# A fifth block of quantized rows, and a piece of that work in every unit of the second attention

## Chip, cores and metric

The kernel is written in Tile, a layer that derives the semaphores from the data flow and plans the order of each engine's instructions itself. It runs on one core of one Trainium2 chip. The metric is the time of one execution on the device, in microseconds (us); a kernel is stated by the median of its runs.

## What is computed

The reference is a two-layer gated Flamingo stack on x of shape (2, 2048, 512), which the kernel sees as 8 blocks of 512 tokens (4 per sequence), each block four tiles of 128 tokens.

```python
x = x + tanh(g_xattn[0]) * L0_xattn(layernorm(x), ctx)   # 16 heads of 32
x = x + tanh(g_ffn[0])   * L0_ffn(layernorm(x))          # 256 routed tokens of a sequence
x = x + tanh(g_xattn[1]) * L1_xattn(layernorm(x), ctx)   # 16 heads of 64: the "second attention"
x = x + tanh(g_ffn[1])   * L1_ffn(layernorm(x))          # the BitNet feed-forward
...
def L1_ffn(x):
    h = bit_linear(x, w1)            # 512 -> 2048: rows to 8-bit integers, weights ternary
    h = silu(depthwise_conv1d(h))    # over neighbouring tokens, kernel of 3
    return bit_linear(h, w2)         # 2048 -> 512: the rows of h to 8-bit integers again
```

What the change touches is the quantization in the last line, that of the "inner rows" h: each token's row of 2048 values is scaled by 127 over its largest absolute value and rounded to integers.

## The kernel before, in words

**The stages in time.** First attention with the router beside it (to about 520 us), the rest of the routed attention and feed-forward (to about 760 us), the second attention (760 to 1560 us), and the second half of the BitNet feed-forward (to the end).

**The second attention** (`cross_attention`, line 218, called on line 1397) is a loop over units (line 353): 16 units u per block n, one unit per head, 128 units and 12 more that empty the pipeline. A unit makes scores (L279), a softmax (maximum on VectorE L119, exponentials on ScalarE L122, reciprocal L130 on VectorE, product L131 on GpSimd), the transposes of the probabilities of two units earlier (L297, copied by VectorE L298), every fourth unit the values (L305) and, in units with u % 4 = 1, the queries of the next group of heads (L256, 16 matmul records, in two chunks that ScalarE moves out, L268). The output projection of a block (L328, moved out by VectorE L339) is spread over eight units of the next block. Each unit ends with a call `beside(u)`, here `beside4` (line 1295).

**What runs beside it.** When a block's attention is done, `stage3_done` (line 1304) queues two generators on the list `stream`: `quantize_rows` and `first_half` (line 1200; the up projection L1179 and the convolution L1189 to L1196, four channel groups k, each ending in a store of the 1 MB tile h to `h_d[g]`, L1227). `first_half` queues `scales_of` (line 1245) on the list `ending`; that computes the rows' scales `hid_s` and, for blocks g below `EARLY`, queues `integers(g)` on the list `later` (L1257). `beside4` takes two steps of `ending` and of `stream` in a unit, and one step of `later` unless u % 4 = 1.

**`integers(g)`** (line 1267) spreads the block's scales over the partitions (four transposes L82 on TensorE, a copy to the single tile `s_b` L1264 on ScalarE) and then takes 16 pieces, one step each. A piece is a column tile of 128x512 of h: a load `hf` from `h_d` (L1272), a product with `s_b` on VectorE (L1279), the rounding, on VectorE in even pieces (L1285, one instruction) and on ScalarE in odd ones (L1282 and L1283, two passes), and a store of the bf16 result to `hq_d[g]` (L1286). The tiles `hf` and `hi` have two buffers each. All of these transfers are issued by SyncE (SP), whose queue is in order.

**The second half** begins when the last block's values are done (`second_half_starts`, line 1344). A loop over blocks g and their tiles i (line 1454) calls `down_and_out` (line 1405): 16 matmuls of `hq` with w2 into one bank of PSUM (L1409), the product with the row's factor and the addition of x on VectorE (L1412), the store. After each tile it takes three steps of `behind`, the generator `quantize_hidden(g + 1)` (line 1355), which provides the integers of the next block. For blocks below `EARLY` these are eight loads from `hq_d` (L1369), whose tiles `hq` have 24 buffers, those of three blocks. For the others `quantize_hidden` does the work of a block in place: 16 loads from `h_d` (L1376; the last block's columns were kept in SBUF), the spreading of the scales, 16 products on VectorE (L1385), 4 roundings on VectorE (L1391) and 12 times two passes on ScalarE (L1388, L1389). The up projection and convolution of the last block, g = 7, are finished in the first three blocks of this loop (`beside4(None, 1)`, line 1477). The two single tokens at the ends of the sequences (`last_tokens`) add 32 matmuls.

```python
def beside4(u, share=2):
    for _ in range(share):
        advance(ending)
        advance(stream)
    if u is None or u % 4 != 1:
        advance(later)
```

The order on each engine is Tile's: it plans with modelled durations, in the order of the program where several instructions are ready. An instruction can stand earlier on its engine than the program has it.

Of the kernel before, what the change touches and what calls it, by code (L numbers as in the profile page):

```python
# [43 lines left out]
def flamingo_kernel(ctx: ExitStack, tc: tile.TileContext, a: dict, out: bass.AP):  # L44
# [1059 lines left out]
    hid_f = const.tile([P, NT], F32, name="hid_f")  # L1104
    h_d = [dramp.tile([P, HC, BLK], F32, name=f"h_d{g}") for g in range(B * NBLK)]
    LAST = B * NBLK - 1
    EARLY = 4
    hq_d = [dramp.tile([P, HC, BLK], BF16, name=f"hq_d{g}") for g in range(EARLY)]
    x3_d = [dramp.tile([S, D], F32, name=f"x3_d{b}") for b in range(B)]

# [134 lines left out]
    def scales_of(g, amax):  # L1245
# [9 lines left out]
        nc.vector.tensor_scalar(hid_f[:, ts(g, TB)], inv, finstep, None, ALU.mult)  # L1255
        if g < EARLY:
            later.append(integers(g))  # L1257
# [9 lines left out]
    def integers(g):  # L1267


        def load(c):  # L1270
            h = act4.tile([P, BLK], F32, name="hf", tag="hf", bufs=2)
            nc.sync.dma_start(out=h, in_=h_d[g][:, c, :])  # L1272
            return h

        s_b, h = scales_spread(g), load(0)
        for c in range(HC):
            behind = load(c + 1) if c + 1 < HC else None
            yield
            nc.vector.tensor_tensor(h, h, s_b, ALU.mult)  # L1279
            q = act4.tile([P, BLK], BF16, name="hi", tag="hi", bufs=2)  # L1280
            if c % 2:
                nc.scalar.activation(h, h, AF.Copy, bias=RND)  # L1282
                nc.scalar.activation(q, h, AF.Copy, bias=-RND)  # L1283
            else:
                nc.vector.tensor_scalar(q, h, RND, RND, ALU.add, ALU.subtract)  # L1285
            nc.sync.dma_start(out=hq_d[g][:, c, :], in_=q)  # L1286
            h = behind

    stream, later = [], []

    def advance(q):
        while q and next(q[0], q) is q:
            q.pop(0)

    def beside4(u, share=2):


        for _ in range(share):
            advance(ending)
            advance(stream)  # L1300
        if u is None or u % 4 != 1:
            advance(later)

    def stage3_done(n, tiles):
        for i, t in enumerate(tiles):
# [49 lines left out]
    def quantize_hidden(g):  # L1355
# [8 lines left out]

        if g < EARLY:
            for k in range(HC // GQ):
# [30 lines left out]
    cross_attention(  # L1397
        W1, act, hold, ps_mm, psum_pool(units, "L1_sc", 3), psum_pool(units, "L1_o", 2), row,
        1, 10, stage3_rows, stage3_done, beside4, second_half_starts,
    )  # L1400
    right1.close()
# [52 lines left out]
    for g in range(LAST + 1):  # L1454
        if g == LAST - 1:
            while stream or ending:
                beside4(None)
            last = last_tokens()
        behind = quantizing[1] if g == 0 else quantize_hidden(g + 1) if g < LAST else iter(())
        for i in range(TB):  # L1460
            t, r, p = ahead.pop(0)
            down_and_out(
                lambda c: hq[g][c // GQ][:, c % GQ, ts(i, P)],
                hid_f[:, g * TB + i : g * TB + i + 1],
                P,
                t,
                out[ds(g // NBLK * S + r, P - p), :],
                p,
                nc.sync if g == LAST else nc.gpsimd,
            )  # L1470
            if g < LAST:
                ahead.append(row_tile(g + 1, i))
            if g >= LAST - 1:
                next(last, None)
            for _ in range(3):
                next(behind, None)
                beside4(None, 1)
# [65 lines left out]
```

## Time and profile before

| | |
|---|---|
| median of the runs | 1743.49 us (3 runs, 1741.15 to 1747.48) |
| the profiled execution | 1741.68 us, its span 1740.0 us |
| mean granted TensorE clock | 0.982 of full speed |
| busy: TensorE matmul, VectorE, ScalarE, GpSimd | 94%, 71%, 63%, 32% of the span |
| second attention, blocks 2 to 6 | 103.8 to 108.3 us each |
| second half, first to last matmul of L1409 | 1563 to 1736 us |

The page of a profile gives first the busy time of each engine, then the span in 40 equal slices (here of 43.5 us) with the busy tenths of each engine, then the DMA queues, the chain of work that ended last, and groups of equal instructions with their mean duration and the idle time in front of them. PE is TensorE's matmuls, PEld its weight loads, DVE VectorE, ACT ScalarE, POOL GpSimd, SP SyncE. The trace behind it answers for single lines, tiles and stretches of time.

### The profile page before, as it was taken

Reading aid. Unit: us, or ns where it says so; the run is one execution under the profiler, and the core shown is the slowest. Engines: PE = TensorE matmul, PEld = TensorE weight load, DVE = VectorE, ACT = ScalarE, POOL = GpSimd, SP = SyncE. Lnnn points to the kernel's source line nnn. Section 1 sums busy time; section 2 is a strip of 40 time slices with the busy share of each in tenths; the row PEclk is TensorE's granted clock in tenths of the full one; section 3 lists DMA queues with packets and bytes.
Section 4 is the critical chain, followed back from the end, with each engine's and each line's share of the span. In section 5 each row is a group of like instructions: output and inputs, shape, how many; then the busy total and the mean of one; then the engine's idle time right before and its main releaser. Section 6 shows DMA issues by size and latency. Waiting matters only on the chain.

```text
span 1740.0 us, 25223 instructions
## 1 busy us (share of the span) xinstructions
PE 1628.8 (94%) x8076; PEld 856.4 (49%) x8122; DVE 1240.6 (71%) x2576; ACT 1103.3 (63%) x3170; POOL 560.1 (32%) x703
## 2 busy tenths in 40 slices
PE   7999888899999989999999999999999999998988
PEld 4545444455555665755454544445444454444433
DVE  5566777865757543345368889898789889877986
ACT  2876566456553333345267878788787887855575
POOL 2534443442340021033223243343332333343221
PEclk9999999999989999999999999999999999999999
DMA  6011111121005851920011334234133233157294
GB/s 222 7 68 56 37 62 68 61 67 55 25 37 197 274 174 63 300 85 25 19 55 73 122 99 148 92 115 164 73 128 115 88 103 132 78 217 264 100 311 149
DMA packets 116973, 196.99 MB, mean 113 GB/s; under 512 B 13117, under 2 KB 51517, under 8 KB 113129
## 3 DMA queue, kind: packets, MB, share of 16 engines
q1 hardware_dynamic: 110664, 177.54, 29.5%
q0 software_dynamic: 5888, 17.83, 3.2%
q8 instruction: 64, 1.05, 0.2%
q14 instruction: 69, 0.56, 0.1%
q10 hardware_dynamic: 288, 0.00, 0.0%
HBM read 120.89 MB, written 74.45 MB: 112 GB/s over the span
## 4 chain that ended last, share of the span: by engine, by line
PE 48%; DVE 27%; ACT 9%; issue 6%; DMA 6%; POOL 3%; SPq 0%; DVEq 0%; POOLq 0%; ACTq 0%
PE pp L328 12%; PE pq L256 9%; DVE h L1196 4%; PE po L305 4%; PE tp L297 4%; PE sc L279 4%; ACT A L122 3%; PE ph L1179 3%; DVE nmx L119 2%; DVE marks L873 2%; DVE u L1190 2%; DVE AT L298 1%; DMA x<-h_d 1%; DVE L_ln_st L99 1%; DMA h_d<-h 1%
## 5 line engine op out<-in xcount | busy, mean ns | idle before, releaser
L122 ACT ACTIVATE A<-sc,nmx 128x128 f32<-128x128 f32 x1024 | 364.7, 386 | 122.6 <-DVE nmx L119 117.9
L131 POOL TENSOR_TENSOR A<-A,rden 128x512 f32<-128x512 f32 x256 | 280.5, 1098 | 493.9 <-DVE rden L130 402.4
L328 PE MATMUL pp<-L_wo,OT 128*128 128x512 f32 x768 | 360.8, 601 | 5.4 <-DVE x L339 5.4
L256 PE MATMUL pq<-xnT,L_wq 128*128 128x512 f32 x768 | 344.8, 596 | 1.3 <-DVE x L339 1.2
L122 ACT ACTIVATION_READ_ACCUMULATOR A<-sc,nmx 128x1 f32 x1024 | 229.5, 224 | 0.0
L256 PEld LDWEIGHTS pq<-xnT,L_wq 128*128 128x128 f32 x768 | 142.5, 191 | 159.7 <-issue 151.4
L119 DVE TENSOR_REDUCE nmx<-sc 128x4 f32<-128x512 f32 x256 | 168.7, 679 | 67.7 <-PE sc L279 67.6
L328 PEld LDWEIGHTS pp<-L_wo,OT 128*128 128x128 f32 x768 | 134.9, 191 | 148.9 <-issue 130.9
L1196 DVE SCALAR_TENSOR_TENSOR h<-u,cw,h 128x512 f32<-128x512 f32 x256 | 197.2, 803 | 5.8 <-ACT h L1192 5.3
L297 PE MATMUL tp<-ident,A 128*128 128x128 f32 x1024 | 164.8, 285 | 23.5 <-POOL A L131 12.4
L297 PEld LDWEIGHTS tp<-ident,A 128*128 128x128 f32 x1024 | 118.6, 143 | 93.2 <-issue 47.5
L298 DVE COPY AT<-tp 128x512 f32<-128x512 f32 x192 | 130.0, 679 | 38.7 <-PE tp L297 38.1
L279 PEld LDWEIGHTS sc<-L_kT,qT 32*128 32x128 f32 (+1 forms) x2048 | 109.7, 189 | 70.8 <-issue 58.2
L279 PE MATMUL sc<-L_kT,qT 32*128 32x128 f32 (+1 forms) x2048 | 136.2, 291 | 3.7 <-ACT A L122 3.1
L1192 ACT ACTIVATE h<-u,cb,cw 128x512 f32<-128x512 f32 x128 | 99.5, 809 | 62.1 <-DVE u L1190 57.1
L305 PE MATMUL po<-AT,L_v 128*32 128x512 f32 (+1 forms) x512 | 120.1, 655 | 11.5 <-DVE AT L298 11.1
L1409 PE MATMUL po<-w2q,hq 128*128 128x512 bf16 x501 | 117.6, 381 | 9.8 <-ACT hq L1389 6.2
L1179 PE MATMUL ph<-xiT,w1q 128*128 128x512 bf16 x477 | 122.5, 379 | 2.1 <-DVE u L1190 0.2
L1190 DVE TENSOR_TENSOR u<-ph,inv_b 128x512 f32<-128x512 f32 x128 | 85.4, 683 | 31.5 <-PE ph L1179 27.7
L130 DVE RECIPROCAL rden<-den 128x4 f32<-128x4 f32 x256 | 43.6, 170 | 80.3 <-ACT A L122 72.7
L1189 POOL COPY u<-carry 128x2 f32<-128x2 f32 x112 | 44.3, 397 | 150.3 <-DVE h L1196 127.7
L1179 PEld LDWEIGHTS <-w1q 128*128 128x128 bf16 x512 | 49.2, 98 | 79.1 <-issue 35.3
(246 smaller groups left out, 2383.1 us busy)
## 6 DMA issues: line engine op xcount, KB each, us to landing
h_d<-h SPq DMA_DIRECT2D x28, 1024.0 KB, 3.9
x_d<-x SPq DMA_DIRECT2D x64, 256.0 KB, 2.0
hf<-h_d SPq DMA_DIRECT2D x64, 256.0 KB, 3.0
x<-h_d SPq DMA_DIRECT2D x48, 256.0 KB, 5.3
x<-in_x SPq DMA_DIRECT2D x32, 256.0 KB, 3.7
x_d<-xo SPq DMA_DIRECT2D x32, 256.0 KB, 2.0
xf<-x_d SPq DMA_DIRECT2D x32, 256.0 KB, 3.5
x<-x_d SPq DMA_DIRECT2D x32, 256.0 KB, 3.4
```

Of the source, the lines that this page charges most:

```text
L119: nc.vector.tensor_reduce(nmx, sc, AX.X, ALU.max, negate=True)
L122: nc.scalar.activation(out_tile[:, h, :], sc[:, h, :], AF.Exp, bias=nmx[:, h : h + 1], accum_out=den[:, h : h + 1],)
L131: nc.gpsimd.tensor_tensor(out_tile, out_tile, rden.unsqueeze(2).to_broadcast([P, n, width]), ALU.mult,)
L256: nc.tensor.matmul(pq, W.wq[:, d, ts(e, P)], xnT[:, d, :], start=(d == 0), stop=(d == DC - 1),)
L279: nc.tensor.matmul(sc[h][:, t, :], qT[e % cpg][r, ts(t, P)], W.kT[r, b, e, :], start=True, stop=True,)
L297: nc.tensor.transpose(tp[:, t, :], A[:, t, :], ident)
L298: copy(AT, tp.rearrange("p t n -> p (t n)"))
L305: nc.tensor.matmul(po[h * dh : (h + 1) * dh, :], W.v[:, b, ts(hd, dh)], AT[c * hpc + h], start=True, stop=True,)
L328: nc.tensor.matmul(pp, OT[e][:, ts(i, P)], W.wo[:, e, :], start=(e == 0), stop=(e == nE - 1),)
L1179: nc.tensor.matmul(ph, w1q[:, d, ts(c, P)], xiT[g][:, d, :], start=(d == 0), stop=(d == DC - 1),)
L1190: nc.vector.tensor_tensor(u[:, 2:], ph, inv_b[g], ALU.mult)
L1196: nc.vector.scalar_tensor_tensor(z, u[:, ds(k, BLK)], cw[:, c, k : k + 1], z, ALU.mult, ALU.add)
```

## The change

One constant is raised and one condition is taken away.

```diff
@@ -1104,7 +1104,7 @@
     LAST = B * NBLK - 1
-    EARLY = 4
+    EARLY = 5
     hq_d = [dramp.tile([P, HC, BLK], BF16, name=f"hq_d{g}") for g in range(EARLY)]
@@ -1298,8 +1298,7 @@
         for _ in range(share):
             advance(ending)
             advance(stream)
-        if u is None or u % 4 != 1:
-            advance(later)
+        advance(later)
```

With `EARLY = 5` block 4 too is quantized by `integers(4)` beside the second attention, by way of `hq_d[4]`, a new tensor in DRAM of 2 MB, and `quantize_hidden(4)` becomes eight loads. With the condition gone, each unit takes a step of `later`, also the units in which queries are made. No tile in SBUF or PSUM changes its size or number.

## Prediction

> **What bounds the kernel now.** I read the page first (busy shares and the 40 slices), then busy time by block of the second attention, then the groups and waits of the last 83 us.
>
> ```profile
> PE 1628.8 (94%) x8076; PEld 856.4 (49%) x8122; DVE 1240.6 (71%) x2576; ACT 1103.3 (63%) x3170; POOL 560.1 (32%) x703
> ...
> PE   7999888899999989999999999999999999998988
> ...
> DVE  5566777865757543345368889898789889877986
> ACT  2876566456553333345267878788787887855575
> ```
>
> TensorE is busy nearly everywhere. VectorE is at 8 or 9 tenths in slices 22 to 35, the second attention, so what is put there must be weighed, not assumed free. The two places of the change are the attention (work added) and the end (work removed).
>
> Busy time for blocks 2 to 6 of the second attention, each window from the first exponential of a block to that of the next:
>
> ```profile
> 901.00:1008.30 107.30, 105.10 (x462) 51.75 (x465) 85.31 (x156) 81.60 (x198) 34.02 (x53) 0.98 0.26 92
> 1008.30:1114.60 106.30, 101.75 (x457) 50.94 (x461) 93.72 (x176) 85.81 (x208) 38.05 (x55) 0.98 0.32 111
> 1114.60:1218.40 103.80, 102.09 (x451) 50.17 (x455) 94.48 (x178) 87.67 (x209) 39.97 (x54) 1.00 0.39 132
> 1218.40:1326.70 108.30, 103.54 (x461) 51.27 (x464) 92.61 (x173) 86.18 (x207) 35.80 (x53) 1.00 0.33 115
> 1326.70:1430.50 103.80, 100.91 (x459) 50.77 (x463) 87.16 (x159) 83.69 (x204) 35.54 (x54) 1.00 0.26 92
> ```
>
> Columns: length, then PE, PEld, DVE, ACT, POOL busy (and count), clock, DMA share, GB/s. And the products of the pieces (L1279) in the same windows, so that one sees how many pieces each block held:
>
> ```profile
> 901.00:1008.30 107.30, 3.78 (x5) 0.98 0.26 92
> 1008.30:1114.60 106.30, 8.67 (x11) 0.98 0.32 111
> 1114.60:1218.40 103.80, 12.51 (x16) 1.00 0.39 132
> 1218.40:1326.70 108.30, 11.00 (x14) 1.00 0.33 115
> 1326.70:1430.50 103.80, 6.18 (x8) 1.00 0.26 92
> ```
>
> PE is busy 97 to 98% of these blocks and its idle time adds up to 16 us in 530. Five pieces or sixteen, the block takes the same: 107.3, 106.3, 103.8, 108.3, 103.8 us for 5, 11, 16, 14 and 8 pieces. The attention is bound by TensorE.
>
> The last 83 us (1657 us to the end) look different:
>
> ```profile
> L1385 DVE TENSOR_TENSOR x<-x,s_b 128x512 f32<-128x512 f32 x48 | 31.2, 687 | 8.2 <-DMA x<-h_d 7.0 <-ACT s_b L1264 0.9 <-ACT hq L1389 0.2
> L1409 PEld LDWEIGHTS <-hq 128*128 128x128 bf16 x268 | 24.0, 98 | 45.1 <-ACT hq L1389 19.0 <-DVE hq L1391 2.8 <-issue 0.4
> ```
>
> There TensorE waits for integers: its weight loads sat idle 19.0 us for ScalarE's rounding and 2.8 us for VectorE's. The copies of `s_b` (L1264) that open the four blocks quantized in place start at 1657.6, 1674.1, 1691.7 and 1709.4 us, so a block costs 16.5 to 17.7 us, while its 64 matmuls need 13.8 (the 32 single-token ones ran in 7.07 us, 0.216 each). Before 1657 us VectorE finishes the convolution of block 7, and TensorE runs blocks 0 to 3 from stored integers: it is at block 4's first weight load at 1660.0 us.
>
> **Part 1, the end: block 4's quantization is removed.** What goes, from the rows above and of L1388, L1389, L1391: 16 products of 0.69 and 4 roundings of 0.42 on VectorE, 24 passes of 0.62 to 0.63 on ScalarE (15 us), one copy of `s_b`, 16 loads of 256 KB in a stretch with a DMA share of 0.84 to 0.94. What comes: 8 loads of 256 KB from `hq_d` (L1369, median 7.1 us to landing). They need the buffers of block 1, free at about 1627 us when TensorE goes on to block 2; the loads of block 3 were issued the same way, over 40 us before use. From 1625 to 1650 us the DMA share is 0.20, so they have room.
>
> Then two limits. The chain of quantization has three links instead of four: block 7's last rounded column, now needed at 1725.4 us, comes 17.7 us earlier, at 1707.7, and with the 10.8 us that TensorE needed after it (1725.4 to 1736.2) that would be 1718.5. TensorE's own work from 1660.0: 256 matmuls and 32, at 0.216, are 62.2 us, and three spreads of scales at 0.49 make 63.7: 1723.7. TensorE is the later one, so **the most that can go is 1736.2 - 1723.7 = 12.5 us**. What is late next: block 6's integers. At full pace block 6 would start at 1660.0 + 27.6 = 1687.6, but its last columns are rounded at about 1692.8 (they follow the products that now end at 1690.5 and 0.69), and its first tile can't end before about 1693 instead of 1691. I take 2 us of loss; **10.5 us go**.
>
> **Part 2, the attention: sixteen pieces are added.** Following the generators, `integers(0)` now runs in units 42 to 58, 1 to 74, 2 to 90, 3 to 106 and 4 to 122, each begun in the unit in which its scales are ready; before, four blocks took units 42 to 127. All fits into the 140 units, so nothing is left for the emptying loop on line 1451. Added: VectorE 16 x 0.682 + 8 x 0.416 = 14.2 us; ScalarE 16 x 0.63 + 0.57 = 10.7 us; TensorE four transposes, 0.6 us; SP 16 x 0.425 + 16 x 0.32 = 11.9 us of issuing, for 6 MB more.
>
> Bounds: above, VectorE's whole 14.2 us, if it set the pace. Below, -3 us, since blocks differ by 4.5 us with no relation to pieces, and another order may fall out better. Between them I compare like with like, units 4 to 7 of each block (convolution, queries and output projection at once), where VectorE is 92 to 98% busy when pieces are there. Without pieces (blocks 2 and 6) 34.3 and 33.6 us; with 5 or 6 pieces (3, 4, 7) 34.4, 35.0, 35.0; block 5, with 6, 39.8. Without block 5 that is 0.85 us for 5.3 pieces, 0.16 each, 2.6 us for 16; with it 0.38 each, 6.1 us. I take **2.6 us**, as the block that held 16 pieces was among the fastest. The cover is TensorE's matmuls; if it is gone, the price is 14.2.
>
> The other edit, a piece in units with u % 4 = 1, adds a wait: an odd piece's two passes (1.26 us) or an even piece's 1.1 us on VectorE stand ahead of the maxima (L119), the exponentials (L122) and the copies of queries (L268) queued behind them, and the next scores wait for those. Such a unit has 16 query matmuls on TensorE (7.1 us in a row at 1248 us), a cover that other units lack, so I cost it at nothing beyond the 2.6; its full price is rival 3. On SP each piece's load and store stand in order with the loads and stores of the attention's rows and of h; a load (median 3.0 us to landing) was awaited 14 times for 17.3 us in all by VectorE, not by TensorE. The transposes of `s_b` now follow the scales at once in five blocks instead of one: in block 0 TensorE idled 0.66 us for it; four more are 2.6 us at most, within the 6.1 above.
>
> A rule that speaks against the change: in this trace 16 of the 78 softmax products on GpSimd (L131) between 985 and 1500 us overlap a piece's product on VectorE, and take 1198 ns instead of 1077. The Trainium skill (GPSIMD Engine Reference, section 1, Specifications) says that GpSimd shares its SBUF interfaces with VectorE and contends with instructions that have two SBUF inputs or use both ports. Row and rule agree; by the row, sixteen more products lengthen GpSimd by 16 x 0.12, some 2 us, at 32% busy; by the rule alone, were GpSimd held for each whole product, 11 us, still beside TensorE.
>
> **Sum.** -10.5 + 2.6 = -7.9 us on the profiled execution's 1741.68: 1733.8. That execution stands 1.8 us below the median of the runs, 1743.49; against the median the same step gives 1735.6, and I forecast 1735.5.
>
> **Rivals.**
> 1. *TensorE is reached in full and the attention charges nothing.* Single-token matmuls fill the wait for block 6, and another order of pieces is as good as that of block 4. For it: 16 pieces in 103.8 us. Against: no block's order repeats. -12.5, down to -15.5 with the -3: 1728 to 1731.
> 2. *The attention takes back most of it.* Stalls like that of block 5's units 4 to 7 (5 us) come once or twice more, or VectorE, at 97% there, gives way. 6.1 to 10 us: net -4.4 to -0.5, 1739 to 1743.
> 3. *Slower: the units with queries become the bound.* Pieces fall in 20 such units (45 to 121). If each holds up the softmax and queries queued behind it by its 1.1 to 1.26 us and TensorE has nothing else to run, 20 x 1.2 = 24 us come in, and 10.5 go: +13.5, 1757; half of it +1.5. It decides from about 0.8 us per unit (+5.2). Against: TensorE's long cover there, and an order planned across units.
> 4. *The change doesn't do what it says:* block 4's stored integers come no earlier than rounded ones. In the second half SP sat 53 us in one wait at L1376, for a buffer, until about 1660. If the eight loads stand behind such a wait, they land 7 us later, TensorE starts block 4 at about 1667, and 10.5 shrinks to 3.5: net -0.9, 1742.6. Against: in the program they come before the loads of block 5.
>
> **How the numbers follow.** About 0.3%, 5.2 us, is what a measurement of this kernel can tell from no change. Forecast 0.45 (its own range 1732 to 1738), rival 1 0.17, rival 2 0.18, rival 4 0.07, rival 3 0.13. Faster is the first two, 0.62; within 0.3% rivals 2 and 4, 0.25; slower rival 3, 0.13. The range leaves out rival 1's lowest end and most of rival 3: 1728 to 1750.
>
> **What would show it.** Right: blocks 3 to 7 of the attention at 104 to 108 us with 14 to 18 products of L1279 each; three `s_b` copies after 1650 us instead of four, 16 to 18 us apart; block 4's 64 matmuls in about 14 us with no wait for ScalarE; last matmul at about 1726 plus what the attention added. Wrong: blocks of the attention over 109 us with VectorE at 95% or more (rivals 2, 3); weight loads of L1409 waiting for `hq_d` loads (rival 4); a first matmul of the second half later than 1563 by more than 6 us.

## The result, and the profile after

The changed kernel takes **1746.97 us** (median of 21 runs) against 1743.49 us, with a ratio of 1.0025 [1.0013, 1.0037]. It is slower by a quarter of a per cent, less than the bound of 0.3% but with an interval that excludes a gain. The forecast was 1735.5, faster. The profiled execution takes 1743.53 us, its span 1741.8 (before: 1740.0), its mean granted clock 0.984. Lines behind L1301 stand one lower than before.

From the page of the changed kernel, busy times and VectorE's slices:

```profile
PE 1633.7 (94%) x8078; PEld 862.3 (50%) x8122; DVE 1246.0 (72%) x2580; ACT 1095.7 (63%) x3162; POOL 564.3 (32%) x703
...
DVE  5566777865667542444368898997989978878886
```

VectorE's total is only 5 us higher: work has moved, as intended. Busy time by block of the second attention, in the same columns as before, each window from the first exponential of a block to that of the next:

```profile
897.40:1003.10 105.70, 103.50 (x463) 51.65 (x465) 85.30 (x156) 81.47 (x199) 34.01 (x53) 1.00 0.26 94
1003.10:1110.80 107.70, 105.11 (x461) 52.55 (x464) 94.89 (x178) 87.44 (x212) 38.48 (x54) 1.00 0.37 126
1110.80:1221.70 110.90, 105.76 (x458) 52.82 (x460) 96.74 (x177) 87.57 (x211) 39.35 (x54) 1.00 0.36 124
1221.70:1330.50 108.80, 104.12 (x455) 51.90 (x458) 97.83 (x181) 87.88 (x212) 38.74 (x55) 1.00 0.37 128
1330.50:1437.00 106.50, 103.85 (x456) 51.41 (x460) 93.80 (x172) 87.27 (x211) 38.08 (x54) 1.00 0.35 119
```

The blocks now hold 6, 16, 16, 17 and 17 products of L1279. They last 105.7 to 110.9 us; before, 103.8 to 108.3. VectorE is at 87 to 90% in the four full ones, no more than the fullest block before (91%). The clock column reads 1.00 everywhere, where two windows of before read 0.98, so two blocks of before were slowed by the clock and none of these was.

The stretches of the two profiled executions, cut at the first query matmul of the second attention, at the first weight load of the second half, and at the last matmul:

| stretch | before | after | difference |
|---|---|---|---|
| second attention | 816.4 | 827.6 | +11.2 |
| of it lost to the halved clock | 10.2 | 5.1 | -5.1 |
| attention without that loss ("net") | 806.2 | 822.5 | +16.3 |
| second half, to its last matmul | 173.0 | 165.8 | -7.2 |

The loss is half the length of the stretches in which the granted clock was 0.5. The attention began 2.3 us earlier in the second trace, and small differences behind the last matmul make up the rest of the +1.8 in the span.

Where in a block the attention has grown is seen when blocks 3 to 6 are cut by units, as the working did it for units 4 to 7 (us net of the clock, summed over the four blocks, and pieces in them):

| units of a block | 0 to 3 | 4 to 7 | 8 to 15 |
|---|---|---|---|
| before | 108.4, 13 pieces | 142.8, 17 | 169.3, 19 |
| after | 109.2, 22 pieces | 140.7, 16 | 184.0, 26 |

So 14.7 of the 16.3 us lie in units 8 to 15 of these blocks. That is where the spread of a block's scales now stands right behind the scales, which before was so in block 2 alone. Before, block 2's units 8 to 15 took 44.9 us and those of blocks 3 to 6 took 42.0 to 43.0, the 42.0 with eight pieces; after, the latter take 44.9 to 47.1, with six or seven.

In the end, the groups of products in place and of weight loads:

```profile
L1384 DVE TENSOR_TENSOR x<-x,s_b 128x512 f32<-128x512 f32 x32 | 20.6, 685 | 4.8 <-DMA x<-h_d 2.5 <-ACT s_b L1264 1.6 <-ACT hq L1388 0.6
L1408 PEld LDWEIGHTS <-hq 128*128 128x128 bf16 x512 | 50.0, 99 | 65.3 <-ACT hq L1388 6.2 <-issue 3.2
```

Sixteen products are gone, and the wait of the weight loads for ScalarE's rounding fell from 19.0 to 6.2 us. The `s_b` copies after 1650 us are three, at 1674.0, 1691.0 and 1707.1. TensorE in the stretch ahead of the first of them:

```profile
1666.84 0.65 PE L1251 MATMUL pm<-ident,amax 128*128 128x128 f32 x4 [0.17 <-DVE amax L1234]
1667.33 6.21 PE L1408 MATMUL po<-w2q,hq 128*128 128x512 bf16 x28
1673.37 0.60 PE L81 MATMUL pb<-ident,hid_s 128*128 128x128 f32 x4
1673.81 13.50 PE L1408 MATMUL po<-w2q,hq 128*128 128x512 bf16 x59
1689.45 0.39 PE L1408 MATMUL po<-w2q,hq 128*128 128x512 bf16 x1 [2.14 <-ACT hq L1388]
```

Here block 5's scales could be spread (`pb`) as soon as block 7's are done (`pm`), but 28 matmuls stand between the two on TensorE. In those 6 us ScalarE stands before its copy of `s_b` (9.9 us in that wait), and at 1689.45 TensorE waits 2.14 us for integers that ScalarE rounds too late.

### The profile page after: what moved, and what is told of

The parts are those of the page before. It is cut to its first block, busy times and chain, and to the rows that moved or that the text cites. A ratio compares the mean times of both kernels' runs of the same rounds, so it can differ in the third digit from the quotient of the medians.

```text
span 1741.8 us, 25266 instructions
## 1 busy us (share of the span) xinstructions
PE 1633.7 (94%) x8078; PEld 862.3 (50%) x8122; DVE 1246.0 (72%) x2580; ACT 1095.7 (63%) x3162; POOL 564.3 (32%) x703
## 4 chain that ended last, share of the span: by engine, by line
PE 50%; DVE 29%; ACT 9%; DMA 5%; issue 3%; POOL 3%; SPq 0%; POOLq 0%; DVEq 0%; ACTq 0%
PE pp L328 10%; PE pq L256 9%; DVE h L1196 5%; PE po L305 4%; ACT A L122 4%; PE tp L297 4%; PE sc L279 3%; PE ph L1179 3%; DVE nmx L119 2%; PE pu L659 2%; DVE marks L873 2%; PE pw L659 2%; PE acc L644 2%; PE po L1408 2%; DVE u L1190 2%
## 5 line engine op out<-in xcount | busy, mean ns | idle before, releaser
L256 PEld LDWEIGHTS pq<-xnT,L_wq 128*128 128x128 f32 x768 | 142.2, 190 | 163.3 <-issue 151.8
L1196 DVE SCALAR_TENSOR_TENSOR h<-u,cw,h 128x512 f32<-128x512 f32 x256 | 192.6, 785 | 2.6 <-ACT h L1192 2.2
L279 PEld LDWEIGHTS sc<-L_kT,qT 32*128 32x128 f32 (+1 forms) x2048 | 114.9, 189 | 73.4 <-issue 57.3
L279 PE MATMUL sc<-L_kT,qT 32*128 32x128 f32 (+1 forms) x2048 | 143.6, 291 | 5.7 <-ACT A L122 5.4
```

The lines of the kernel that those rows point to most:

```text
L256: nc.tensor.matmul(pq, W.wq[:, d, ts(e, P)], xnT[:, d, :], start=(d == 0), stop=(d == DC - 1),)
L279: nc.tensor.matmul(sc[h][:, t, :], qT[e % cpg][r, ts(t, P)], W.kT[r, b, e, :], start=True, stop=True,)
L1196: nc.vector.scalar_tensor_tensor(z, u[:, ds(k, BLK)], cw[:, c, k : k + 1], z, ALU.mult, ALU.add)
```

## The experiments

Two traces show where the time is, not why the attention is longer. These theories are named by letters in what was expected. **N**: the number of pieces, whose work is charged wherever it stands. **P**: their place in the last units of a block (in the last pair of runs, P is the plan). **Q**: the units with queries. **S**: scales spread at once. **F**: blocks with more than 12 pieces. **L**: the late spread in the end, above. **R**: score matmuls taken apart. **W**: small waits. **V**, **A**: the pieces' work on VectorE, on ScalarE. **O**: the order and waits that come with a step, whatever its work.

All results; ratios are to the kernel before on the same chip, stretches are from one profiled execution each:

| run | median us, ratio [95%] | attention, lost, net | second half |
|---|---|---|---|
| e1_rate4 | 1749.13, 1.0042 [1.0020, 1.0064] | 822.3, 5.1, 817.2 | 178.0 |
| e2_count5 | 1747.53, 1.0045 [1.0022, 1.0068] | 814.2, 6.8, 807.4 | 182.9 |
| e3_later_spread | 1742.17, 1.0004 [0.9975, 1.0032] | 830.3, 15.4, 814.9 | 167.0 |
| e4_not_12to15 | 1747.72, 1.0038 [1.0017, 1.0059] | 827.9, 5.1, 822.8 | 168.5 |
| e5_not_query | 1765.20, 1.0139 [1.0095, 1.0183] | 843.8, 15.4, 828.4 | 170.1 |
| e6_other_rest | 1749.98, 1.0052 [1.0035, 1.0069] | 826.3, 13.7, 812.6 | 174.4 |
| e7_gpsimd_product | 1778.91, 1.0215 [1.0180, 1.0249] | 860.1, 30.7, 829.4 | 167.7 |
| e8_spread_earlier | 1747.01, 1.0039 [1.0017, 1.0061] | 825.7, 5.1, 820.6 | 162.9 |
| e9_paired_scores | 1746.59, 1.0032 [1.0013, 1.0051] | 829.0, 8.5, 820.5 | 168.6 |
| e10_before_paired | 1739.37, 0.9995 [0.9977, 1.0012] | 814.1, 8.5, 805.6 | 174.6 |
| e11_later_and_earlier | 1741.20, 1.0003 [0.9985, 1.0020] | 822.6, 8.5, 814.1 | 163.3 |
| e12_all_three | 1743.02, 1.0008 [0.9992, 1.0023] | 827.8, 13.7, 814.1 | 164.8 |
| e13_no_product | 1737.74, 0.9970 [0.9953, 0.9987] | 821.1, 11.9, 809.2 | 169.3 |
| e14_one_pass | 1734.22, 0.9937 [0.9900, 0.9975] | 815.9, 5.1, 810.8 | 166.3 |
| e15_neither | 1744.17, 1.0010 [0.9997, 1.0024] | 828.4, 11.9, 816.5 | 164.9 |
| e16_before_neither | 1741.86, 1.0008 [0.9990, 1.0025] | 816.7, 6.8, 809.9 | 171.6 |
| e17_fixed_order | 1852.80, 1.0639 [1.0610, 1.0668] | 952.3, 59.7, 892.6 | 152.1 |
| e18_before_fixed | 1840.46, 1.0579 [1.0550, 1.0609] | 925.6, 49.5, 876.1 | 160.1 |

Where the attention's plan is that of another kernel, two executions agree within 2 us net: e8 with after (820.6, 822.5), e11 with e3 (814.1, 814.9), and e2, whose plan is nearly that of before (807.4, 806.2).

**The two halves of the change, one at a time.** The rate alone is the changed kernel with four early blocks; the count alone is the kernel before with five.

```diff
-    EARLY = 5
+    EARLY = 4
```

> The changed kernel with EARLY back at 4: the rate alone, 64 pieces, one in each unit from 43 to 106, and block 4 quantized in place again. Measure: the attention from its first query weight load to the first weight load of L1409, 816.3 us before and 827.6 after; the end from there to the last matmul, 173.0 and 165.8. Theory N (number: each piece charges VectorE's and ScalarE's time, wherever it stands): 64 pieces as before, so 814 to 819 us, end 173, total as before. Theory P (place: pieces in the short units 12 to 15 of a block, where ScalarE and VectorE have no cover, hold up the scores): 823 to 828, total 7 to 11 us over the kernel before. Theory S (the spread of scales that now follows the scales at once stalls the block's end): four instead of five of those, 822 to 826.

```diff
-    EARLY = 4
+    EARLY = 5
```

> The kernel before with EARLY at 5: the number alone, 80 pieces at three in four units; what does not fit is taken by the emptying loop. Attention 816.3 before, 827.6 after. Theory N: 826 to 831, as the changed kernel. Theory P and theory S: 815 to 820, because pieces still miss every fourth unit and the spreads of blocks 1 to 4 come long after their scales; then the end as in the changed kernel or some us longer for the last pieces, and the total 3 to 7 us below the kernel before.

The step in every unit costs 11.0 of the 16.3 us net by itself, without one piece more; its 822.3 us fall into S's range (822 to 826) and just short of P's. Its second half took 178.0 us, 5 more than before with the same work, which was not followed up. The count alone tested less than meant: of its sixteen pieces, twelve came after the attention, into the second half (first weight load to block 7's scales 109.7 us instead of 93.9). That the attention didn't change there says nothing on N.

**Where the steps stand.** The changed kernel with no step in units 12 to 15 of a block, or none in the units with queries, other units taking two; and the kernel before with the resting unit moved.

```diff
-        advance(later)
+        for _ in range(1 if u is None else (1, 1, 2, 0)[u // 4]):
+            advance(later)
```

> The changed kernel with no piece in units 12 to 15 and two in units 8 to 11: same 80 pieces, same 16 per block, other places. Theory P: attention 816 to 821, total 4 to 9 us below the changed kernel. Theory N: 827, no change. Theory S: 826 to 829, or worse, since units 10 and 11 then hold two pieces beside the spread.

```diff
-        advance(later)
+        for _ in range(1 if u is None else (1, 0, 1, 2)[u % 4]):
+            advance(later)
```

> The changed kernel with no piece in units with u % 4 = 1 and two in units with u % 4 = 3: again 16 pieces in a block of units. Measure: the attention from its first query weight load to the first weight load of L1409, less the time lost to the halved clock: 806 us before, 822 after, 817 with four blocks at the changed rate, 807 with the old rate. Theory Q (query units: it is the pieces in units with queries that hold up TensorE): 806 to 812. Theory F (full: up to some 12 pieces in a block ride free, each one more is paid with about 0.8 us, wherever it stands): 819 to 826.

```diff
-        if u is None or u % 4 != 1:
+        if u is None or u % 4 != 3:
```

> The kernel before (four blocks, 12 pieces in a block of units) with the free unit moved: pieces in units u % 4 = 0, 1 and 2, none in u % 4 = 3. Attention net of the halved clock 806 before. Theory Q: 811 to 818, since a third of the pieces now stands in query units. Theory F: 804 to 809.

P falls: 822.8 net without the steps at the block ends. F's numbers were missed twice. Q stays undecided: without steps in the query units the attention is longer still (828.4, in a kernel of two runs whose units u % 4 = 3 take two pieces), but in e6 the same twelve pieces a block, moved into query units, cost 6.4 net, and its 812.6 lie in Q's range (811 to 818).

**Later spreads, and another engine.** A delay of six steps ahead of the first block's pieces, so that later blocks' spreads wait in the list instead of following their scales at once; and the product of a piece on GpSimd.

```diff
+        if g == 0:
+            later.append(iter(range(6)))
         later.append(integers(g))
```

> The changed kernel with the first spread six units later, so that all five spreads fall in unit 0 of a block instead of unit 10, six units after their scales; same 80 pieces, same rate. Theory S: the stalls at the blocks' ends go, attention 816 to 820, total 5 to 9 us below the changed kernel. Theory P and theory N: 825 to 829, no change.

```diff
-            nc.vector.tensor_tensor(h, h, s_b, ALU.mult)
+            nc.gpsimd.tensor_tensor(h, h, s_b, ALU.mult)
```

> The changed kernel with the pieces' product (L1279 of before) on GpSimd instead of VectorE: 80 x 0.68 us leave VectorE, about 80 x 1.05 to 1.1 us come to GpSimd, which is at 35%. Theory F with VectorE as the engine that is full: attention net 806 to 812, total 5 to 10 us below the changed kernel. Theory F with ScalarE as the full engine, or theory Q by ScalarE's passes: 819 to 825. If GpSimd's softmax products, queued behind the pieces, become the bound: over 826.

The delay takes 7.6 of the 16.3 us net away, with the same 80 pieces; units 8 to 15 of blocks 3 to 6, now without a spread, take 174.3 us instead of 184.0. In that execution the halved clock took 10 us more, so the raw attention is no shorter and S's 816 to 820 were missed; the median of the runs is 4.8 us lower than the changed kernel's, on another chip (its ratio of 1.0004 has an interval that holds the changed kernel's 1.0025). Taking products off VectorE (78 to 81% busy in the blocks instead of 87 to 90%) makes everything worse, but it is no clean test of VectorE's occupancy. VectorE's roundings now stand 32.5 us in 13 waits for GpSimd's products, and TensorE waits 18.8 us for VectorE's copies of transposed probabilities and 23.9 for its rows `xi`, where it waited 0.7 and 5.5 in the changed kernel. The softmax products, which the third case expected to be late, held TensorE up by 0.9 us.

**The end.** Block 5's spread is started while block 3 runs.

```diff
+            if g == EARLY - 2 and i == 0:
+                started = quantize_hidden(EARLY)
+                next(started)
...
+        if g == EARLY - 1:
+            behind = started
```

> The changed kernel with block 5's loads and the spreading of its scales traced in block 3 of the second half instead of block 4. In the changed kernel the last maximum's transposes are at 1666.8 us but block 5's s_b is copied only at 1674.0, behind 28 matmuls on TensorE, and the last matmul comes 70.5 us after those transposes, where the forecast had 67. Theory L (late spread: this is what the forecast of the end missed): s_b for block 5 within 2 us of VectorE's last maximum, transposes to last matmul 66.5 to 68.5, total 2 to 4 us below the changed kernel. Rival (TensorE is full there anyway): 70 to 71, no change. The attention stays at 822 net in both.

TensorE in this run, at the same place as above:

```profile
1663.94 0.66 PE L1251 MATMUL pm<-ident,amax 128*128 128x128 f32 x4 [0.18 <-DVE amax L1234]
1664.43 0.60 PE L81 MATMUL pb<-ident,hid_s 128*128 128x128 f32 x4
1664.87 20.02 PE L1408 MATMUL po<-w2q,hq 128*128 128x512 bf16 x90
```

The spread follows the scales, and 90 matmuls run without a wait. The second half is 162.9 us instead of 165.8, from block 7's scales to the last matmul 68.1 instead of 70.5. L is shown in the profile, also in e11 and e12 below, which have the same edit (68.9 and 69.7 us; 70.5 to 74.3 in the eleven kernels that quantize block 4 early without it). The medians (1747.01, 1746.97) don't show it.

**Torn pairs.** In the planned kernels TensorE's order shows a tempting cause. Weight loads of scores at the end of a block, before, then after:

```profile
1198.18 0.75 PEld L279 LDWEIGHTS sc<-L_kT,qT 64*128 64x128 f32 x12 [0.81 <-issue]
```

```profile
1200.19 0.20 PEld L305 LDWEIGHTS po<-AT,L_v 128*64 128x64 f32 x4 [0.17 <-issue]
1201.20 0.30 PEld L279 LDWEIGHTS sc<-L_kT,qT 64*128 64x128 f32 x4 [0.81 <-issue]
...
1202.21 0.74 PEld L279 LDWEIGHTS sc<-L_kT,qT 64*128 64x128 f32 x6 [0.17 <-issue]
```

Twelve in 0.75 us before, six in 0.74 after. Two score matmuls of 64 rows each start together when they are neighbours: of 1024 weight loads in the trace of before, 436 stand under 30 ns ahead of the next (such two are a pair here), after 392. The next kernels pin the order of the score matmuls of a unit: in the changed kernel, in the kernel before, and in the changed kernel with the later and the earlier spread (e12), with e11 as the same without pinning.

```diff
-                    nc.tensor.matmul(
+                    ins = nc.tensor.matmul(
...
+                    if not bias and (t or h):
+                        tc.keep_in_program_order(ins)
```

> The changed kernel with the score matmuls of the second attention pinned in program order, so that the matmuls of the two heads of a chunk, which use different halves of TensorE's rows, mostly follow each other again (the plan of the changed kernel tears them apart: 392 score weight loads start under 30 ns before the next one in the second attention, 436 before). Theory R (torn pairs: each costs about 0.1 us): over 425 such pairs, attention (first query weight load to first weight load of L1409, 827.6 us in the changed kernel, 822.5 net of the halved clock) shorter by 4 to 6, total 3 to 6 us below the changed kernel's 1.0025 of the kernel before. Theory W (the pairs are a sign, the time goes into waits for ScalarE and VectorE at the blocks' ends): at most 2 us shorter.

> The kernel before with the same pinning of the scores. Control: its pairs are nearly whole (436), so by theory R nothing changes: attention within 2 us of 816.4, total within 3 us. If pinning has a price of its own, it shows here.

> The changed kernel with both remedies: the spreads of the attention six units later (alone: attention net 814.9 instead of 822.5, 432 pairs, but 15.4 us lost to the halved clock instead of 5.1) and block 5's spread in the second half a block earlier (alone: 68.1 us from the last maximum's transposes to the last matmul instead of 70.5). If the two add up: net time about 10 us below the changed kernel and 3 us below the kernel before; by the clock, if it is halved as often as with the later spread alone, total 0 to 4 us below the kernel before, else 5 to 8.

> Later spreads, the earlier spread in the second half, and the pinned scores together. Theory R: the pairs were whole with the later spreads already, so the pinning adds nothing: within 3 us of the run without it. Theory W: the same. It is tried as the best version: 0 to 8 us below the kernel before.

R falls. Pinned, the changed kernel has 452 pairs, more than the kernel before, and its attention is 820.5 net, 2 us less than unpinned, as W had it (2 at most); the kernel before goes to 467 pairs and gains 0.6. With the pairs restored, TensorE's idle time in the attention goes up from 29.3 to 34.5 us: a torn pair filled time in which TensorE would have waited. e11 has e3's plan of the attention and repeats it; e12 has another, and the two agree at 814.1 net. So the later spread takes 8 us off with the changed kernel's free order and 6.4 with pinned scores (e12 against e9). None of these four beats the kernel before beyond its interval.

**The work taken out of the pieces, the steps left in.** Most of the scaling (e13), the first of ScalarE's two passes (e14), or both (e15, and e16 in the kernel before) are done on 8 of 512 columns and left out for the rest.

```diff
-            nc.vector.tensor_tensor(h, h, s_b, ALU.mult)
+            nc.vector.tensor_tensor(h[:, :8], h[:, :8], s_b[:, :8], ALU.mult)
...
-                nc.scalar.activation(h, h, AF.Copy, bias=RND)
+                nc.scalar.activation(h[:, :8], h[:, :8], AF.Copy, bias=RND)
```

> The changed kernel, in which a piece's product on VectorE takes 8 of its 512 columns, so that most of the integers are rounded from unscaled rows: this part of the computation is left out. Some 80 products of 0.68 us become about 0.1, 46 us less on VectorE; loads, stores, spreads and the number of steps stay. Theory V (VectorE's work of the pieces lengthens the attention): 0.6 us off for each of 16 more pieces is 9 us, and at least 9 of the net 822.5 us of the attention go, 806 to 813. Theory O (the order and the waits that come with a step cost, not its work): 818 to 825 net.

> The changed kernel, in which the first of the two passes on ScalarE in an odd piece takes 8 columns, so that the integers of odd columns are not rounded properly: this part of the computation is left out. 40 passes of 0.62 us become about 0.2, 17 us less on ScalarE in the attention. Theory A (ScalarE's work lengthens it, since the exponentials, queries and copies queue behind the passes): 5 to 10 us of the net 822.5 go. Theory V or O: 819 to 825 net.

> The two edits before together: the product on 8 columns and the first pass on 8 columns, so neither scaling nor proper rounding is computed for the rest. Work (V and A): the attention falls to 800 to 808 net, the time of the kernel before or less, though the steps and spreads are those of the change. O: 815 to 825 net.

> The same two edits in the kernel before, whose attention has 64 pieces: the scaling and the proper rounding are left out. Work (V and A): its 806.2 us net too lose 0.1 to 0.2 us per piece, 794 to 801. O: 804 to 809 net, and the difference between this run and the changed kernel with the same edits stays at 10 to 16 us.

Each alone takes 12 to 13 us off the attention, and with either the change would be faster than the kernel before. e13 lies in V's range (806 to 813), e14 beyond A's. Both together take off only 6, and the kernel before gets 3.7 us longer with less to do; the difference between the two kernels is then 6.6 us net (816.5 against 809.9) instead of 16.3. So neither V nor A is a price per microsecond of work that adds up: every edit draws a new plan, and plans for the same or less work differ by several microseconds. Nor is work ruled out as part of the cause. The spreads still come at once in e13 and e15, and units 8 to 15 of blocks 3 to 6 take only 176.4 and 175.5 us there instead of 184.0, which suggests that it is the spread together with the full work behind it that makes them long.

**The same order for both.** The last pair removes TensorE's plan from the comparison. Every matmul and transpose of the second attention, and of what runs beside it, is kept in the program's order on TensorE. The two sequences in the attention then differ only by the spreads `pb`: those of blocks 1, 2 and 3 stand later without the change, and block 4's is not there. VectorE and ScalarE keep a planned order; apart from the pieces, 66 of VectorE's 1108 instructions and 33 of ScalarE's 1485 stand in another place.

```diff
+def pe_order(op):
+    def issue(*args, **kw):
+        ins = op(*args, **kw)
+        if KEEP:
+            KEEP[0].keep_in_program_order(ins)
+        return ins
+    return issue
...
-                    nc.tensor.matmul(
+                    pe_order(nc.tensor.matmul)(
```

> The changed kernel with every matmul and transpose of the second attention, and of what runs beside it, kept in the order of the program on TensorE. The level may be anywhere (an order not planned: 800 to 860 us net); what counts is the difference from the kernel before with the same edit, run beside it. Theory P (the plan): the attention is 0 to 5 us longer than there, and with 7 to 10 us less in the end the changed kernel is the faster of the two, by 3 to 10 us. Theory O (the steps cost by themselves, as waits): 10 to 16 us longer, and the changed kernel is the slower one by 2 to 8 us, as without the edit.

> The kernel before with the same edit: its TensorE order in the attention is then that of the changed kernel's run but for the places of four transposes of scales. Theory P: 0 to 5 us shorter in the attention than the changed kernel with this edit, in total 3 to 10 us slower. Theory O: 10 to 16 us shorter, in total 2 to 8 us faster.

P falls, and O's 10 to 16 us are just passed: no difference in TensorE's plan is needed for the loss. The attention is 16.5 us net longer with the change (892.6 against 876.1). That the planned kernels differ by 16.3 is no proof of one and the same cause: here all of it is idle time of TensorE (133.4 against 117.0 us), while in the planned kernels idle time goes up by only 3.2 us (26.1 to 29.3) and the rest stands as busy time of a changed order. The changed kernel is 12.3 us slower in the medians and 14.6 in the profiled executions: in these the halved clock adds 10.2 to the attention, the second half gives 8.0 back, and the attention began 4.1 us earlier. What TensorE waited for in the attention (engine, tile, what it waited for: us, times, longest us; line numbers are 13 higher, and TensorE's instructions all stand on the helper's line 44). With the change:

```profile
PE po L44 <- ACT OT L326: 36.0, 12, 3.8
PE po L44 <- DVE AT L311: 33.0, 27, 2.4
PE ptr L44 <- ACT xnT L258: 25.8, 12, 5.3
PE pb L44 <- DVE hid_s L1139: 11.8, 5, 2.5
PE ph L44 <- ACT xiT L1177: 8.9, 6, 2.1
...
PE pt L44 <- DVE xi L1170: 3.2, 4, 1.4
```

Without it:

```profile
PE po L44 <- ACT OT L326: 30.3, 15, 3.7
PE ptr L44 <- ACT xnT L258: 28.3, 12, 5.4
PE po L44 <- DVE AT L311: 25.4, 24, 2.4
PE pt L44 <- DVE xi L1170: 9.3, 11, 1.7
PE ph L44 <- ACT xiT L1177: 5.9, 5, 1.8
...
PE pb L44 <- DVE hid_s L1139: 2.3, 1, 2.3
```

The spreads wait 11.8 us in five times instead of 2.3 in one: **+9.5**. The value matmuls `po` wait 7.6 us more for VectorE's copies of transposed probabilities and 5.7 more for ScalarE's copies of their results, the up projection `ph` 3.0 more; 6.1 and 2.5 are saved at `pt` and `ptr`. All rows of this view sum to 130.7 against 113.8 us. One of the spreads, with the change, then the same place without it:

```profile
1127.58 0.60 PE L44 MATMUL pm<-ident,amax 128*128 128x128 f32 x4
1130.51 0.62 PE L44 MATMUL pb<-ident,hid_s 128*128 128x128 f32 x4 [2.33 <-DVE hid_s L1139]
```

```profile
1128.43 0.60 PE L44 MATMUL pm<-ident,amax 128*128 128x128 f32 x4
1128.87 0.60 PE L44 MATMUL tp<-ident,A 128*128 128x128 f32 x4
```

Between `pm` and `pb` VectorE takes the maximum and computes the scales. Where the spread is the next thing on TensorE, it stands 2.33 us; where the spread waits in the list behind other pieces, TensorE goes on. Matched instruction by instruction, net of the clock, the changed kernel falls back by 2.4 to 3.0 us at each of the four spreads behind the first (11.3 in all, their transposes included) and by 7.2 in the one block that has 16 pieces against 5; in each of the other blocks it moves by -2.4 to +1.8.

## Why the prediction was wrong

**The step that failed** is the price of the attention, "I take 2.6 us": it measured +11.2, or +16.3 with the clock's loss taken out of both, beyond every value in the working but the whole 14.2 of VectorE's work and rival 3's 12 to 24. The 0.16 a piece came from units 4 to 7, and these have not grown at all (142.8 and 140.7 us); the time came in units 8 to 15, which the working did not price. It failed in two parts.

- **The spread.** "In block 0 TensorE idled 0.66 us for it; four more are 2.6 us at most." With equal order one costs 2.3 us, the four more 9.5. In the planned kernel the wait is hardly seen as such (1.8 us in three spreads; 0.7 to 1.1 us each in e5, e13 and e14), as other instructions stand there, but delaying the spreads gives 7.6 net back (e3, and 8.4 in e11 with the same plan), and the time went into the units where they stand. The 0.66 was itself the wait that was left after the plan had filled it; the 44.9 us of block 2's units 8 to 15 were there to be read. This part was left out of the sum, as lying within the bound of 6.1.
- **The pieces.** About 7 us of the 16.5 remain. In the fixed order they are waits of the value matmuls for copies on VectorE and ScalarE, engines that were 72 to 80% and 67 to 71% busy there, so 0.4 us a piece where the working took 0.16 (and had 0.38 as the other reading). That a block with 16 pieces was "among the fastest" was in part the luck of its plan: e16 makes that very block 109.0 us net, from query to query, instead of 104.1, with less work in it. A single block of a planned kernel is no measure of a price.

**Point by point.** TensorE was not 97 to 98% busy in the five blocks, as the working read its rows, but 96 to 98%. The end: 10.5 us were to go, 7.2 went; from block 7's scales to the last matmul 8.6. The two limits were right in kind (three spreads, block 4's matmuls without a wait, the last integers late), and the missing 2 to 3 us are block 5's spread behind 28 matmuls, which the working didn't see: with it in place (e8) that part is 68.1 us, against 79.1 - 10.5 = 68.6 as forecast. Rival 1 fell with the attention. Rival 2 had the attention take back most of the gain, 10 us at most where 11.2 came (16.3 without the clock); its stall of block 5's units 4 to 7 did not come back (35.8 us at most there after, 39.8 before). Rival 3 was nearest in the total (1745 for the half of it), but whether by its mechanism, the query units, is open: e5 speaks against it, e6 for it. Rival 4 fell: the last of block 4's eight loads landed at 1644.3 us, more than 20 us before its matmuls.

**The forecast's own tests** called it: a block over 109 us, "wrong", was there (110.9), but with VectorE at 87%, not 95%, and the first matmul of the second half came 9 us later, not under 6.

**What stays open.** How a planned kernel's 16 us split between spreads and pieces can't be said finer than the scatter of the plans, some 4 us either way (809.2, 810.8, 816.5 for three kernels with the same steps and less work). Why e5 and e6 are so much longer was not followed up. The two causes in e17 are shown for the program's order on TensorE; for the planned order only the spread was tested by itself, e3 delays all pieces by six units as well, and how the time came to stand as busy time is shown only for the torn pairs.

## What to carry to other kernels

Work that hides in an engine's idle tenths still moves that engine's short answers, the copies and scales that the bound engine waits for, so price it by those waits and not by the busy share, and in all units of a block, not only in the busiest. A step that makes the bound engine wait for a chain across engines (here transpose, maximum, scale, transpose) was cheap here when it came some units late and dear when it came at once. Where a planner orders the work, compare two kernels under one fixed order before a difference of 1% is given a cause: here blocks within one plan, and two plans, scattered by as much.

## What was not expected of the hardware

The granted clock fell to a half inside the busy attention, for multiples of 3.41 us by the trace's clock records, before mostly at block ends, where small transposes and waits stand close together. Windows of before, each half-clock one after the 3.4 us ahead of it (PE's busy time is the second number, the clock follows POOL's):

```profile
997.90:1001.30 3.40, 2.26 (x19) 1.84 (x20) 3.40 (x7) 2.76 (x10) 0.27 (x1) 1.00 0.75 219
1001.30:1004.70 3.40, 3.40 (x5) 0.42 (x4) 2.66 (x7) 2.38 (x13) 1.31 (x1) 0.50 0.73 228
1103.70:1107.10 3.40, 1.86 (x22) 1.24 (x19) 2.74 (x7) 1.03 (x2) 0.62 (x1) 1.00 0.45 122
1107.10:1110.50 3.40, 3.21 (x16) 1.81 (x16) 3.26 (x7) 2.57 (x13) 0.00 (x0) 0.51 0.56 187
```

TensorE was busy 66% and 55% of the stretch ahead, far from idle. How much of the attention this takes depends on the plan: 5.1 us after, 10.2 before, 30.7 in e7, 59.7 in e17, where TensorE waits most. By and large, more idle time on TensorE went with more lost to the clock (26.1 us idle in the attention of before, 29.3 after, 58.4 in e7, 133.4 in e17), and the 15.4 us lost in e3 hid what it gave back. The Trainium skill (TensorE: Matmul & The Clock Gate, Part 1, What's actually happening) gives two states, half and full, and a window of 3413 ns that runs freely, and our trace agrees with both (the half-clock stretches of the two rows begin 105.81 us apart, 31 such windows); it ties the half state to an idle window, and here it followed windows with TensorE busy for over half of their length, with single waits of 1.16 us at most.

Score matmuls with 64 rows were the other surprise: neighbours' weight loads stand 7 ns apart and the next pair's 105 ns, so that a torn pair takes twice as long on the trace (six loads in 0.74 us, above), and yet restoring 60 pairs was worth 2 us.
